# A shared expert cut at two and a half blocks of tokens, with its third block's first inner values kept on chip

## The chip, the cores and the metric

The kernel runs on one core of one Trainium2 chip. The metric is the device time of one execution in microseconds; the figure for a kernel is the median of its runs. A profile is one further execution, recorded by the hardware profiler. The core has five engines with a queue of instructions each: PE (matrix multiply; the profile shows its weight loads apart, as PEld), DVE (vector), ACT (scalar functions), POOL (GpSimd) and SP (it issues DMAs here). [...]

## The reference

Two layers, each with a residual: attention over 2 × 1024 tokens of width 256, and then a mixture of experts. The change lies in the second:

```python
def _L0_ffn_ref(hidden_states, gate_w, shared_gate_w, w13, w2, se_gate_up_w, se_down_w):
    ...
    gu = x @ se_gate_up_w.T
    I_sh = se_down_w.shape[1]
    shared = jax.nn.silu(gu[:, :I_sh]) * gu[:, I_sh:] @ se_down_w.T
    shared = shared * jax.nn.sigmoid(x @ shared_gate_w.T)
    logits = x @ gate_w.T
    probs = jax.nn.softmax(logits.astype(jnp.float32), axis=-1)
    weights, sel = jax.lax.top_k(probs, TOP_K)
    ...
    return (shared + sparse).reshape(orig_shape)
...
x = x + _L0_attn_ref(_layernorm(x, axis=-1), ...)
x = x + _L0_ffn_ref(_layernorm(x, axis=-1), ...)
```

`sparse` is the sum over 60 routed experts (inner width 176), each token going to its best 4 of them. The shared expert (inner width 704) takes every token. All of it is fp32.

## The kernel before

The 2048 tokens are 16 tiles of 128. After attention and routing, the mixture of experts runs in three stages on PE:

1. **First half of the shared expert** (the loop at L1095), for the tokens 0 to 1023, while routing of the last tiles still runs beside it.
2. **Routed experts** (L1173 to L1201): 60 experts in turn. Each reads its rows from `xg` in HBM (`rows_of`, the tile `xe`), is transposed on PE (`tpe`, copied by DVE to `xT`), multiplied (`up`, `second`), and its rows are scattered to `yt` in HBM by POOL (`send_back`, L884).
3. **The tail**, the second half of the shared expert (the loop at L1271), for the tokens 1024 to 2047. Beside it, `gather(i)` loads the four routed results of tile i (`got`, an SP DMA of 512 KB at L1263) and adds them to `acc` by four DVE instructions (L1265). Finished tiles go to the output.

The shared expert works on blocks of 512 tokens (`FB`), four in all, and `shared` takes two of them per call. For one block, `ups` makes the inner values `hs` in 6 chunks of 128 (`NC2`): two groups of matmuls per chunk (the last chunk is half as wide and needs one), 11 groups in all (L814, tile `sg`); ACT takes the silu of the first (L824), and DVE multiplies it by the second (L826). `downs` then multiplies `hs` by the second weight, for four tiles of 128 tokens (L836, tile `so`), and DVE adds each result, weighted, to `acc` (L844). Each `yield` is a step: PE has issued one group of `sg`, or one of `so`. The order for blocks a and b is ups(a), ups(b), downs(a), downs(b): 30 steps. `sg` has two PSUM buffers for each of its two halves, and `so` has two.

What else the steps carry: in the first half, the pieces of work in `later` and then `weighs` are taken up one per step for the first 22 steps, and then two per step. A piece of `later` is one scatter of a token tile's rows to `xg`: a DVE instruction makes the indices (L685), then POOL issues the indirect DMA (L690). A piece of `weighs` is four DVE instructions (L711). The last 16 scatters and 4 pieces of `weighs` fall into this loop. Expert row loads wait for all scatters. In the tail, `gather` is called in steps 4, 6, 7, 9, 10, 12, ..., two steps of every three.

The order on PE, DVE, ACT and POOL is that of the code (a manual schedule) in the first half; in the routed experts ACT, DVE and SP are manual, and in the tail PE and DVE. A manual engine takes its instructions in the order in which the Python code issues them, so that an instruction that waits holds up all behind it. What is left is put in order by a scheduler.

The pools of SBUF are two stacks, left and right, and a pool that closes gives its place to the next. In the first half `hs` has two buffers in `sw` on the left; in the tail two buffers in `sw2` on the right.

```python
        for r, _ in enumerate(shared(blocks[:half], sw, ps_sg, ps_so)):
            ...
            for _ in range(1 if r < 2 * (2 * NC2 - 1) else 2):
                if later or weighs and r >= 12:
                    (later or weighs).pop(0)()
...
        for r, _ in enumerate(shared(blocks[half:], sw, ps_sg, ps_so)):
            if r >= 4 and todo and r % 3 != 2:
                i = todo.pop(0)
                gather(i)
```

Of the kernel before, what the change touches and what calls it, by code (L numbers as in the profile page):

```python
# [1 line left out]

# [14 lines left out]
P = 128  # L17
B, T, C = 2, 1024, 256
NT = B * T // P
# [3 lines left out]
CC = C // P  # L23
# [4 lines left out]
NC2 = -(-ISH // P)  # L28
# [5 lines left out]
FB = 512  # L34
# [17 lines left out]
def attention_moe_kernel(  # L52
# [15 lines left out]
    nc = tc.nc  # L68
# [14 lines left out]
    acc = const.tile([P, NT, C], F32, name="acc")  # L83
# [35 lines left out]
    ends_of, ends_s = pool("ends", 1, "right")  # L119
# [96 lines left out]
    sg = const.tile([P, NT], F32, name="sg")  # L216
# [5 lines left out]
    start = const.tile([P, E], F32, name="start")  # L222
# [13 lines left out]
    ps_misc, ps_misc_s = pool("ps_misc", 1, space=PSUM)  # L236
# [281 lines left out]
    later = []  # L518
    exps = []
    weighs = []  # L520
# [279 lines left out]

    added = []

    def shared(blocks, sw, ps_sg, ps_so):


        def ups(n, hs):
            for m in range(NC2):
                last = m == NC2 - 1
                ps = []
                for part in range(1 if last else 2):  # L810
                    p = ps_sg.tile([P, FB], F32, tag=f"sg{part}", name=f"sg{n}_{m}_{part}")
                    c0 = (2 * m + part) * P
                    for c in range(CC):
                        nc.tensor.matmul(  # L814
                            p,
                            lhsT=ws1_sb[:, c, c0 : c0 + P],
                            rhs=x2T[:, c, n * FB : (n + 1) * FB],
                            start=c == 0,
                            stop=c == CC - 1,
                        )  # L820
                    ps.append(p)
                    if part == 0:
                        r = 64 if last else P
                        nc.scalar.activation(hs[0:r, m, :], p[0:r, :], AF.Silu)  # L824
                    if last or part == 1:
                        nc.vector.tensor_mul(  # L826
                            hs[0:r, m, :], hs[0:r, m, :], p[64:P, :] if last else p
                        )
                    yield

        def downs(n, hs):
            for t in range(FB // P):
                i = n * (FB // P) + t
                po = ps_so.tile([P, C], F32, tag="so", name=f"so{i}")
                for m in range(NC2):
                    nc.tensor.matmul(  # L836
                        po,
                        lhsT=hs[:, m, t * P : (t + 1) * P],
                        rhs=ws2_sb[:, m, :],
                        start=m == 0,  # L840
                        stop=m == NC2 - 1,
                    )
                added.append(
                    nc.vector.scalar_tensor_tensor(  # L844
                        acc[:, i, :], po, sg[:, i : i + 1], acc[:, i, :], ALU.mult, ALU.add
                    )
                )
                yield

        ahead = None  # L850
        for n in blocks:
            hs = sw.tile([P, NC2, FB], F32, tag="hs", name=f"hs{n}")
            nc.gpsimd.memset(hs[64:P, NC2 - 1, :], 0.0)
            yield from ups(n, hs)
            if ahead is not None:
                yield from downs(*ahead)
            ahead = (n, hs)
        yield from downs(*ahead)


    def up(xT, w, h, n, ps_gu, name):
# [85 lines left out]
    with tc.manual_schedule(engines={mybir.EngineType.PE}), ExitStack() as both:  # L947
# [46 lines left out]
        ahead = scores(*order[0])  # L994
        for r, (b, qb, jp, jj, s) in enumerate(order):
            if r == R // B:
# [6 lines left out]
                fc, fc_s = pool("fc", 1, "left")  # L1003
                xs = fc.tile([P, NT, XR], F32, name="xs")
                nc.gpsimd.memset(xs[:, :, C:XR], 0.0)
                x2T = fc.tile([P, CC, NT * P], F32, name="x2T")
                ws1_sb = fc.tile([P, CC, 2 * ISH], F32, name="ws1_sb")
                nc.sync.dma_start(ws1_sb, ws1.rearrange("(c p) n -> p c n", p=P))
                ws2_sb = fc.tile([P, NC2, C], F32, name="ws2_sb")
                nc.sync.dma_start(ws2_sb, ws2.rearrange("(c p) n -> p c n", p=P))  # L1010
                rw, rw_s = pool("rw", 2, "left")
# [6 lines left out]
            if r + 1 < R:  # L1018
                ahead = scores(*order[r + 1])
# [9 lines left out]
            for g in range(NKV):  # L1029
                nc.tensor.matmul(  # L1030
                    av[32 * g : 32 * g + 32, :],
                    lhsT=vaug[:, b * TPB + s, g, H * jj : H * jj + 32],
                    rhs=es[g // 2][:, g % 2, :],
                    start=s == 0,
                    stop=s == TPB - 1,
                )
            if s == TPB - 1:
                group_end(av, encT, jp, jj)
                if jp == 1 and jj == 1:
                    for t in range(0, QB // P, 2):  # L1040
                        i = (b * T + qb * QB) // P + t
# [15 lines left out]
        ps_m2, ps_m2_s = pool("ps_m2", 1, space=PSUM)  # L1057
        turns = [0]

        def bank(n, name):  # L1060
            turns[0] += 1
            of = (ps_misc, ps_m2)[turns[0] % 2]
            return of.tile([P, n], F32, tag="misc", name=name)

        sw, sw_s = pool("sw", 2, "left")
        ps_sg, ps_sg_s = pool("ps_sg", 2, space=PSUM)
        ps_so, ps_so_s = pool("ps_so", 2, space=PSUM)
# [22 lines left out]
        went = [False, False]  # L1090
        sp_s = ExitStack()
        sp_s.enter_context(tc.manual_schedule(engines={mybir.EngineType.SP}))
        blocks = range(NT * P // FB)
        half = len(blocks) // 2
        for r, _ in enumerate(shared(blocks[:half], sw, ps_sg, ps_so)):  # L1095
            if ends:
                fill(R + r)

            for k, steps in enumerate(rest):
                if r >= 3 + 3 * k and next(steps, R) == R:  # L1100
                    went[k] = True
            if all(went):
                next(ranked, None)
            for _ in range(1 if r < 2 * (2 * NC2 - 1) else 2):
                if later or weighs and r >= 12:
                    (later or weighs).pop(0)()
        assert not ends and all(went) and next(ranked, R) == R
        for piece in later + weighs:
            piece()
        sp_s.close()  # L1110
        both.close()
        rk_s.close()
        for s in (ps_so_s, ps_sg_s, ps_m2_s, ps_misc_s, sw_s, rw_s, ends_s):
            s.close()


# [56 lines left out]
        with tc.manual_schedule(  # L1173
# [12 lines left out]
            ahead = None  # L1186
            for k, r in enumerate(turn_of):
                h = hbuf[k % 3]
                up(xTs.pop(k), ws[k], h, CAPS[r], ps_gu, f"{r}")
                last = (r, ws[k], h, xes.pop(k))  # L1190
# [4 lines left out]
                ahead = last  # L1195
# [57 lines left out]


    gw, gw_s = pool("gw", 6, "right")
    sw, sw_s = pool("sw2", 2, "right")
    ps_sg, ps_sg_s = pool("ps_sg2", 2, space=PSUM)
    ps_so, ps_so_s = pool("ps_so2", 2, space=PSUM)

# [8 lines left out]

    with tc.manual_schedule(engines={mybir.EngineType.PE, mybir.EngineType.DVE}):
        todo = list(range(NT))  # L1270
        for r, _ in enumerate(shared(blocks[half:], sw, ps_sg, ps_so)):  # L1271
            if r >= 4 and todo and r % 3 != 2:
                i = todo.pop(0)
                gather(i)
                if i < TPB and i % 2:
                    nc.scalar.dma_start(ot[:, i - 1 : i + 1, :], acc[:, i - 1 : i + 1, :])
        for i in todo:
            gather(i)
    for i in range(TPB, NT):
        nc.sync.dma_start(ot[:, i, :], acc[:, i, :])  # L1280
    for s in (ps_so_s, ps_sg_s, sw_s, gw_s, fc_s):
        s.close()


# [70 lines left out]
```

## Time and profile before

| | us |
|---|---|
| median of 3 runs | 686.99 (686.0 to 687.66) |
| the profiled execution | 687.18 |
| its span | 685.1 |
| first matmul of `downs` in the first half | at 402.71 |
| first transpose of a routed expert | at 425.60 |
| first matmul of the tail | at 622.81 |
| first addition of a gathered tile (L1265) | at 631.80 |
| last DVE addition (L844) | at 681.61, takes 0.48 |

The span is what the profiler shows from the first to the last instruction; the execution's own time is 2.1 us longer. Times "at" are microseconds from the span's start. In the profile a line such as `acc<-so,sg,acc` names the tile that is written and those that are read; "x96" counts records, of which a matmul in fp32 leaves several; and what stands after `<-` behind an idle time is what ended the wait. The end of a matmul is modelled in the profile, and the profile's word for a releaser that it can't name is "remote".

### The profile page before, as it was taken

To read this page: it belongs to the slowest core of one execution; us is meant where nothing else is said; L and a number is where in the kernel's file an instruction comes from. 1 tells how busy PE (TensorE), PEld (TensorE's weight loads), DVE (VectorE), ACT (ScalarE), POOL (GpSimd) and SP (SyncE) were. 2 spreads that over 40 slices of the span, in tenths; PEclk is the share of its full clock that TensorE was granted. 3 is DMA by queue.
4 is the path that set the end of the run, shared out by engine and by line. 5 is a ranking of instruction groups with operands and counts; after the bars stand their busy time and mean duration, and the time that the engine had idled before them with its cause. 6 is when DMAs were issued, how large, how long until landed. Compare 5 with 4: busy or idle time off the path is not lost. (4 is left out here: it accounts for less than half of the span.)

```text
span 685.1 us, 12519 instructions
## 1 busy us (share of the span) xinstructions
PE 669.6 (98%) x4194; PEld 380.5 (56%) x4195; DVE 367.6 (54%) x1403; ACT 356.7 (52%) x499; POOL 190.2 (28%) x259
## 2 busy tenths in 40 slices
PE   8899999999999999999999998999999999999997
PEld 8433333332224323233225567998898889985466
DVE  4656684823035286446648764444454445443884
ACT  2567787779987687867872510333333333332110
POOL 5020100200000034433045253344544455443000
PEclk9999999999999999999999999999999999999999
DMA  8999930030000011111011076698989888933951
GB/s 283 289 284 298 333 101 1 1 132 1 1 1 1 1 42 50 66 49 59 0 58 58 16 261 229 206 290 293 311 281 295 285 287 299 293 110 105 306 178 52
DMA packets 64275, 106.33 MB, mean 155 GB/s; under 512 B 7417, under 2 KB 51209, under 8 KB 64210
## 3 DMA queue, kind: packets, MB, share of 16 engines
q1 hardware_dynamic: 55010, 86.57, 39.0%
q0 software_dynamic: 7680, 17.32, 7.4%
q10 hardware_dynamic: 1520, 1.64, 0.7%
q8 instruction: 33, 0.54, 0.3%
q14 instruction: 32, 0.26, 0.2%
HBM read 64.13 MB, written 42.45 MB: 156 GB/s over the span
## 5 line engine op out<-in xcount | busy, mean ns | idle before, releaser
L496 PE MATMUL sc<-qT,kT 32*128 32x512 f32 x1024 | 159.8, 639 | 1.9 <-DVE qT L479 0.9
L511 ACT ACTIVATE ex<-sc,rqk 128x1024 f32<-128x1024 f32 x128 | 134.4, 1111 | 37.8 <-PE sc L496 36.2
L1030 PE MATMUL av<-ex,vaug 128*32 128x512 f32 x1024 | 137.3, 604 | 2.0 <-DVE den L537 1.3
L511 ACT ACTIVATE ex<-sc 128x1024 f32<-128x1024 f32 x128 | 124.0, 1021 | 28.9 <-PE sc L496 26.0
L884 POOL DMA_INDIRECT yt<-ys,dst x96 | 93.0, 969 | 115.2 <-ACT ys L1169 75.9
L496 PEld LDWEIGHTS sc<-qT,kT 32*128 32x128 f32 x1024 | 52.4, 183 | 110.1 <-issue 68.6
L1162 PE MATMUL ye<-w,hbuf 128*128 128x256 f32 (+5 forms) x384 | 93.3, 381 | 0.0
L690 POOL DMA_INDIRECT xg<-xs,idx x64 | 63.3, 989 | 93.9 <-DVE idx L685 68.6
L814 PE MATMUL sg<-x2T,ws_sb 128*128 128x512 f32 x176 | 78.1, 596 | 1.1 <-ACTq L1240 1.1
L868 PE MATMUL gua<-xT,w 128*128 128x128 f32 (+5 forms) x480 | 73.2, 295 | 0.5 <-DVE xT L1150 0.5
L868 PEld LDWEIGHTS gua<-xT,w 128*128 128x128 f32 x480 | 70.1, 191 | 4.9 <-issue 0.6
L1169 ACT COPY ys<-ye 128x256 f32<-128x256 f32 (+5 forms) x60 | 29.9, 499 | 75.6 <-PE ye L1162 62.1
L1162 PEld LDWEIGHTS ye<-w,hbuf 128*128 128x128 f32 (+5 forms) x384 | 58.9, 164 | 14.5
L876 DVE TENSOR_TENSOR hbuf<-hbuf,gua 128x128 f32<-128x128 f32 (+5 forms) x60 | 18.9, 315 | 82.5 <-ACT hbuf L875 35.1
L1030 PEld LDWEIGHTS av<-ex,vaug 128*32 128x32 f32 x1024 | 20.4, 107 | 76.5 <-issue 66.7
L814 PEld LDWEIGHTS sg<-x2T,ws_sb 128*128 128x128 f32 x176 | 32.6, 190 | 38.9 <-issue 35.8
L875 ACT ACTIVATE hbuf<-gua 128x128 f32<-128x128 f32 (+5 forms) x60 | 18.0, 299 | 59.8 <-PE gua L868 44.6
L824 ACT ACTIVATE hs<-sg 128x512 f32<-128x512 f32 (+1 forms) x24 | 14.3, 597 | 59.2 <-PE sg L814 57.0
L424 POOL TENSOR_TENSOR t<-u,rope_sb 128x128 f32<-128x128 f32 x32 | 16.9, 558 | 99.1 <-DVE u L412 61.7
L836 PE MATMUL so<-ws_sb,hs 128*128 128x256 f32 x192 | 42.5, 381 | 1.5 <-DVE acc L844 1.5
L868 PE MATMUL gub<-xT,w 128*112 128x128 f32 (+5 forms) x240 | 41.2, 294 | 0.0
L836 PEld LDWEIGHTS so<-ws_sb,hs 128*128 128x128 f32 x192 | 36.2, 190 | 8.2 <-DVE acc L844 2.2
(182 smaller groups left out, 679.0 us busy)
## 6 DMA issues: line engine op xcount, KB each, us to landing
w<-in_wexp_dram SPq DMA_DIRECT2D x60, 624.0 KB
xg<-void SPq DMA_DIRECT2D x60, 221.0 KB
yt<-zero SPq DMA_DIRECT2D x32, 256.0 KB
got<-yt SPq DMA_DIRECT2D x16, 512.0 KB
xe<-xg SPq DMA_DIRECT2D x24, 136.0 KB
xe<-xg SPq DMA_DIRECT2D x10, 170.0 KB
yt<-ys,dst POOLq DMA_INDIRECT x96
xe<-xg SPq DMA_DIRECT2D x8, 187.0 KB
```

What stands on the lines that cost most here:

```text
L496: nc.tensor.matmul(sc[:, gg, :], lhsT=kT[b][r : r + 32, s0 : s0 + P], rhs=qT[b][r : r + 32, j, t0 : t0 + QB], start=True, stop=True,)
L511: nc.scalar.activation(ex, sc, AF.Exp, scale=rqk[:, 1, i : i + 1] if b == 0 else 1.0)
L690: s = nc.gpsimd.indirect_dma_start(out=xg[:, :], out_offset=bass.IndirectOffsetOnAxis(ap=at_, axis=0), in_=xs[:, i, :], in_offset=None, bo ...
L814: nc.tensor.matmul(p, lhsT=ws1_sb[:, c, c0 : c0 + P], rhs=x2T[:, c, n * FB : (n + 1) * FB], start=c == 0, stop=c == CC - 1,)
L836: nc.tensor.matmul(po, lhsT=hs[:, m, t * P : (t + 1) * P], rhs=ws2_sb[:, m, :], start=m == 0, stop=m == NC2 - 1,)
L868: nc.tensor.matmul(ps[part][0:m, 0:n], lhsT=w[:, c * W1C + c0 : c * W1C + c0 + m], rhs=xT[:, c, 0:n], start=c == 0, stop=c == CC - 1,)
L875: nc.scalar.activation(h[:, 0, 0:n], ps["ga"][:, 0:n], AF.Silu)
L876: nc.vector.tensor_mul(h[:, 0, 0:n], h[:, 0, 0:n], ps["ua"][:, 0:n])
L884: s = nc.gpsimd.indirect_dma_start(out=yt[:, :], out_offset=bass.IndirectOffsetOnAxis(ap=at, axis=0), in_=y, in_offset=None, bounds_check= ...
L1030: nc.tensor.matmul(av[32 * g : 32 * g + 32, :], lhsT=vaug[:, b * TPB + s, g, H * jj : H * jj + 32], rhs=es[g // 2][:, g % 2, :], start=s == 0,
L1162: nc.tensor.matmul(po[:, t, :], lhsT=h[:, k, t * rows : (t + 1) * rows], rhs=w[:, CC * W1C + k * C : CC * W1C + (k + 1) * C], start=k == 0 ...
L1169: nc.scalar.copy(ys, po)
```

## The change

`shared` is taken apart into two generators, `ups(n, chunks, ps_sg, sw)` and `downs(n, ps_so)`, which find the inner values of block n in `hs_of[n]`. The loops chain them by hand:

- First loop: ups(0), ups(1), downs(0), the first three chunks of ups(2) (six groups), downs(1): 36 steps. `later` and `weighs` are taken up one per step to the end.
- Second loop: the last three chunks of ups(2) (five groups), ups(3), downs(2), downs(3): 24 steps. `gather` is called in steps 4, 6, 7, 8, 9, 10, 12, ..., five steps of every six.

The values of block 2 lie in a pool of their own, `kept`, that stays open on the right from the first loop to the end. For it the pool `ends` stays open too, so that the pools of the routed experts start at another place. `sw2` has one buffer, for block 3. The computation, its instructions and its DMAs are the same in number and size.

```diff
+    hs_of = {}
+
+    def ups(n, chunks, ps_sg, sw):
+
+        if n not in hs_of:
+            hs = hs_of[n] = sw.tile([P, NC2, FB], F32, tag="hs", name=f"hs{n}")
+            nc.gpsimd.memset(hs[64:P, NC2 - 1, :], 0.0)
+        hs = hs_of[n]
+        for m in chunks:
...
+    def downs(n, ps_so):
+        for t in range(FB // P):
...
-        ahead = None
-        for n in blocks:
-            hs = sw.tile([P, NC2, FB], F32, tag="hs", name=f"hs{n}")
-            nc.gpsimd.memset(hs[64:P, NC2 - 1, :], 0.0)
-            yield from ups(n, hs)
-            if ahead is not None:
-                yield from downs(*ahead)
-            ahead = (n, hs)
-        yield from downs(*ahead)
...
+        kept, kept_s = pool("kept", 1, "right")
         sw, sw_s = pool("sw", 2, "left")
...
-        blocks = range(NT * P // FB)
-        half = len(blocks) // 2
-        for r, _ in enumerate(shared(blocks[:half], sw, ps_sg, ps_so)):
+
+        part = range(NC2 // 2), range(NC2 // 2, NC2)
+        steps_of = chain(
+            ups(0, range(NC2), ps_sg, sw),
+            ups(1, range(NC2), ps_sg, sw),
+            downs(0, ps_so),
+            ups(2, part[0], ps_sg, kept),
+            downs(1, ps_so),
+        )
+        for r, _ in enumerate(steps_of):
...
-            for _ in range(1 if r < 2 * (2 * NC2 - 1) else 2):
-                if later or weighs and r >= 12:
-                    (later or weighs).pop(0)()
+            if later or weighs and r >= 12:
+                (later or weighs).pop(0)()
...
-        for s in (ps_so_s, ps_sg_s, ps_m2_s, ps_misc_s, sw_s, rw_s, ends_s):
+        for s in (ps_so_s, ps_sg_s, ps_m2_s, ps_misc_s, sw_s, rw_s):
...
-    sw, sw_s = pool("sw2", 2, "right")
+    sw, sw_s = pool("sw2", 1, "right")
...
-        for r, _ in enumerate(shared(blocks[half:], sw, ps_sg, ps_so)):
-            if r >= 4 and todo and r % 3 != 2:
+        steps_of = chain(
+            ups(2, part[1], ps_sg, kept),
+            ups(3, range(NC2), ps_sg, sw),
+            downs(2, ps_so),
+            downs(3, ps_so),
+        )
+        for r, _ in enumerate(steps_of):
+            if r >= 4 and todo and r % 6 != 5:
...
```

More of the change, by code (lines that the diff above doesn't have):

```diff
@@ L1 @@
 from contextlib import ExitStack
+from itertools import chain
 import concourse.bass as bass
@@ L801, in attention_moe_kernel @@
     added = []
-    def shared(blocks, sw, ps_sg, ps_so):
-        def ups(n, hs):
-            for m in range(NC2):
[L808 to L846, printed above, removed]
-                )
-                yield
-        ahead = None
-        for n in blocks:
-            hs = sw.tile([P, NC2, FB], F32, tag="hs", name=f"hs{n}")
-            nc.gpsimd.memset(hs[64:P, NC2 - 1, :], 0.0)
-            yield from ups(n, hs)
-            if ahead is not None:
-                yield from downs(*ahead)
-            ahead = (n, hs)
-        yield from downs(*ahead)
@@ new lines, in attention_moe_kernel @@
+    hs_of = {}
[5 more added lines that the diff above has]
+        for m in chunks:
+            last = m == NC2 - 1
+            ps = []
+            for part in range(1 if last else 2):
+                p = ps_sg.tile([P, FB], F32, tag=f"sg{part}", name=f"sg{n}_{m}_{part}")
+                c0 = (2 * m + part) * P
+                for c in range(CC):
+                    nc.tensor.matmul(
+                        p,
+                        lhsT=ws1_sb[:, c, c0 : c0 + P],
+                        rhs=x2T[:, c, n * FB : (n + 1) * FB],
+                        start=c == 0,
+                        stop=c == CC - 1,
+                    )
+                ps.append(p)
+                if part == 0:
+                    r = 64 if last else P
+                    nc.scalar.activation(hs[0:r, m, :], p[0:r, :], AF.Silu)
+                if last or part == 1:
+                    nc.vector.tensor_mul(
+                        hs[0:r, m, :], hs[0:r, m, :], p[64:P, :] if last else p
+                    )
+                yield
@@ new lines, in downs @@
+    def downs(n, ps_so):
+        for t in range(FB // P):
+            i = n * (FB // P) + t
+            po = ps_so.tile([P, C], F32, tag="so", name=f"so{i}")
+            for m in range(NC2):
+                nc.tensor.matmul(
+                    po,
+                    lhsT=hs_of[n][:, m, t * P : (t + 1) * P],
+                    rhs=ws2_sb[:, m, :],
+                    start=m == 0,
+                    stop=m == NC2 - 1,
+                )
+            added.append(
+                nc.vector.scalar_tensor_tensor(
+                    acc[:, i, :], po, sg[:, i : i + 1], acc[:, i, :], ALU.mult, ALU.add
+                )
+            )
+            yield
@@ L1092, in attention_moe_kernel @@
         sp_s.enter_context(tc.manual_schedule(engines={mybir.EngineType.SP}))
-        blocks = range(NT * P // FB)
-        half = len(blocks) // 2
-        for r, _ in enumerate(shared(blocks[:half], sw, ps_sg, ps_so)):
+        part = range(NC2 // 2), range(NC2 // 2, NC2)
[5 more added lines that the diff above has]
+            downs(1, ps_so),
+        )
+        for r, _ in enumerate(steps_of):
             if ends:
@@ L1270, in attention_moe_kernel @@
         todo = list(range(NT))
-        for r, _ in enumerate(shared(blocks[half:], sw, ps_sg, ps_so)):
-            if r >= 4 and todo and r % 3 != 2:
+        steps_of = chain(
[3 more added lines that the diff above has]
+            downs(3, ps_so),
+        )
+        for r, _ in enumerate(steps_of):
+            if r >= 4 and todo and r % 6 != 5:
                 i = todo.pop(0)
@@ L1280, in attention_moe_kernel @@
         nc.sync.dma_start(ot[:, i, :], acc[:, i, :])
-    for s in (ps_so_s, ps_sg_s, sw_s, gw_s, fc_s):
+    for s in (ps_so_s, ps_sg_s, sw_s, gw_s, kept_s, ends_s, fc_s):
         s.close()
```

## The prediction

> **What bounds the kernel now.** I read the page first, then the chain of waits, then busy time by stage, then the waits and the order of time at the two places that the diff touches.
>
> ```profile
> span 685.1 us, 12519 instructions
> PE 669.6 (98%) x4194; PEld 380.5 (56%) x4195; DVE 367.6 (54%) x1403; ACT 356.7 (52%) x499; POOL 190.2 (28%) x259
> PE sg L814 6%; PE so L836 3%; DVE acc L844 0%
> ```
>
> PE, the matmul engine, is busy 98% of the span, and the chain that ends last is only the tail: L814 and L836 back to back. So the time moves in two ways alone: PE idles less somewhere, or it is made to wait somewhere new. Busy time in three stretches (the end of the shared expert's first half, the routed experts, the tail):
>
> ```profile
> core 0: us, PE busy (x) PEld busy (x) DVE busy (x) ACT busy (x) POOL busy (x), PEclk, DMA share, GB/s
> 402.70:425.80 23.10, 21.62 (x99) 18.14 (x98) 10.92 (x55) 0.59 (x1) 9.79 (x10) 1.00 0.84 302
> 425.80:621.70 195.90, 195.17 (x1296) 174.95 (x1294) 90.34 (x469) 65.07 (x179) 90.17 (x93) 1.00 0.80 259
> 622.80:681.70 58.90, 58.75 (x184) 34.88 (x184) 40.98 (x84) 7.17 (x12) 2.90 (x4) 1.00 0.56 180
> ```
>
> The routed experts leave PE 0.7 us of idle in 196: nothing to win there. The tail leaves it none, but DVE already works 41.0 of 58.9 us. The first stretch, eight `so` groups, has holes. Its waits:
>
> ```profile
> DVE acc L844 <- PE so L836: 7.9, 4, 3.7
> DVE acc L844 <- remote: 3.7, 1, 3.7
> PEld so L836 <- DVE acc L844: 2.2, 2, 1.9
> PE so L836 <- DVE acc L844: 1.5, 1, 1.5
> ```
>
> Two PSUM buffers hold `so`; a group may start when the DVE addition (L844) two groups earlier is done. The order of time shows these additions going late:
>
> ```profile
> 410.97 0.48 DVE L844 SCALAR_TENSOR_TENSOR acc<-so,sg,acc 128x256 f32<-128x256 f32 x1 [2.26 <-PE so L836]
> ...
> 415.28 0.48 DVE L844 SCALAR_TENSOR_TENSOR acc<-so,sg,acc 128x256 f32<-128x256 f32 x1 [3.68 <-remote]
> ...
> 419.62 0.48 DVE L844 SCALAR_TENSOR_TENSOR acc<-so,sg,acc 128x256 f32<-128x256 f32 x1 [3.72 <-PE so L836]
> ...
> 420.16 5.60 PE L836 MATMUL so<-ws_sb,hs 128*128 128x256 f32 x24 [1.48 <-DVE acc L844]
> ```
>
> In the tail a `so` group takes 20.73/8 = 2.59 us (in the chain of waits 96 records, eight groups, take 20.73). Counted from 402.71, group 4 ends near 413.1 and group 5 near 415.7, but their additions start at 415.28 and 419.62: they hear of them 2 to 4 us late. In just this time the DMA share is 1.0 and over (8 expert weights of 624 KB and ten scatters). The eight groups need 20.72 us and run from 402.71 to about 425.76, so 2.33 us are lost.
>
> [...] Here the last scatter ends on POOL at 418.38 and the row load that waits for it issues at 420.06: 1.7 us. [...] L826 measures 686 ns, and I use the trace's values.
>
> **The change, part by part.** Everything before 402.71 keeps its order on every engine.
>
> *Moved PE work.* Six groups of `ups(2)` leave the tail for the place between downs(0) and downs(1). A group costs 38.03/22 = 1.729 us (L814 x88, 4 records each), so 10.37 us are added in the middle and 10.37 leave the tail: PE's sum is unchanged.
>
> *The hole in the middle.* The two late signals belong to the last `so` of block 0 and the first of block 1. Between these now stand 10.37 us of matmuls that need neither buffer, so the 2.33 us go. What is late next: if silu of the first moved group also hears of it only at 419.6, its PSUM buffer comes free at about 420.2 (0.6 us of ACT), and PE wants it at 402.71 + 10.36 + 4 × 1.729 = 419.99. I take 0.3 us for this; bounds 0 and 2.3 (the same lateness landing on a buffer that is wanted at once). Downs(1) then comes after the DMA rush, with additions 2.6 us apart and at most 1.3 us of weighing (L711) between them: no wait.
>
> *Scatters.* One per step instead of two. POOL spends 0.98 us on each at a pitch of 1.28. The last index now stands on DVE behind the product of the second moved pair (PE end 420.0, product 0.7), so the last scatter issues near 421, lands near 423.3, and the row loads (`xe`) issue 3.2 us later than now. Before, they issued at 420.06 and the transposes that read them ran at 425.60, right behind the last `so`: at most 5.5 us to land. PE wants them after downs(1), near 433.9. Cost 0, hidden by 5 us. On SP the register load of the overflow count now stands ahead of these loads; its input is ready at 404.87, SP is idle until 420: 0. On POOL the three clears of `hbuf` and one of the kept `hs` (about 0.5 us each, as L853) move between scatters that wait for indices anyway: 0, at worst 2 us of those 5. The 0.50 us before the first `gua` stays, and the experts keep their order and their 8 weights already loaded: 0.
>
> *The tail.* Put T = 0 at its first matmul (622.81 before). DVE's pitches in the tail: a gather's four additions 1.957 us (eight in 646.32 to 650.23), a product 0.60, an addition of `so` 0.40:
>
> ```profile
> 646.32 4.00 DVE L1265 SCALAR_TENSOR_TENSOR acc<-got,wk,acc 128x256 f32<-128x256 f32 x8
> 650.23 0.68 DVE L826 TENSOR_TENSOR hs<-hs,sg 128x512 f32<-128x512 f32 x1
> 650.83 2.04 DVE L1265 SCALAR_TENSOR_TENSOR acc<-got,wk,acc 128x256 f32<-128x256 f32 x4
> ```
>
> The same 16 gathers must now fit a tail 10.4 us shorter, five in six steps. They can't start earlier: they wait for the routed experts' last scatter, and the first was added at 631.80, T + 8.99. Walk through it. The last kept group ends at 5 × 1.729 = 8.64, silu 0.65 and product 0.60 end at 9.97, and gather 0 runs to 11.92. The next product waits for PE until 12.17, and from there DVE does not rest: nine gathers (17.61), six products (3.60) and the first `so` addition (0.40) end at 33.78. PE has 16 × 1.729 + 2 × 2.59 = 32.84 us of work before it needs that buffer, so it waits 1.0 us. Afterwards DVE has 12 us of work in 13.6 and keeps up. PE ends at 33.84 + 6 × 2.59 = 49.4, the last addition (0.5) at 49.9. Walked in the same way, the kernel before ends at 59.2, with no wait; measured 59.28. So the tail shrinks by 9.3 to 9.4, not 10.37. Bounds of the new wait: 0.5 us if a gather takes 1.90, 1.9 if it takes 2.05 (its records without overlap). Loads don't limit: six are in flight, and at 350 GB/s (636 to 642 us) 512 KB take 1.5 us. The last output DMA is as before.
>
> *Sum.* Middle +10.37 − 2.33 + 0.3 = +8.3, tail −9.35: −1.0 us. The profiled execution took 687.18 us (2.1 around its span), which gives 686.2; it lies 0.19 above the median 686.99, so against that 686.0.
>
> **Rivals.** *DVE keeps pace:* the late signals vanish and the tail wait is nil, because gathers overlap better or the first ones start on loads that have landed sooner; −2.3: 684.7 us. For it: the walk puts only 1 us of wait, on one buffer. Against: DVE would be busy nearly all of 38 us. *The lateness moves:* what delays the signals is the DMA rush, and silu and product of the moved groups hear late too, with PSUM buffers two deep as well; middle saves nothing, tail loses 1.0: about 688.0 us, no change that can be measured. Against: these buffers are wanted 4 groups, 6.9 us, after the late moment. *DVE sets the end (slower):* the tail's gathers stand in front of products and additions in a FIFO. If gather 0 can be added later than T + 10, every further us is a us that PE waits for `so`; at T + 13.2 the wait is 4.0 us and the total 689.0 us. It decides from about T + 12.6. For it: the `hs` of block 3 and `got` now lie in memory that the experts have just used, with longer lists of waits. Against: before it was T + 8.99, with the same chain of scatters ahead.
>
> **How the numbers follow.** A measurement of this kernel tells about 0.2% (1.4 us) from no change: faster is below 685.6, slower above 688.4. My case 0.42, its own range 685.0 to 687.2 from the bounds of the two waits, of which 0.12 lies below 685.6. DVE keeps pace 0.30, lateness moves 0.13, DVE sets the end 0.15. Faster 0.42, same 0.43, slower 0.15. The range reaches from below the second case to above the third: 684.0 to 688.4.
>
> **What would show it.** Right: between the first downs and the first transpose of the experts PE has under 0.5 us of idle; the experts begin 8.0 to 8.6 us later and last as long as before; in the tail PE waits about 1 us, once, for an L849 addition at the third or fourth of the eight `so` groups, behind gathers. Wrong: PE waits on `sg` in the middle, `xe` that lands after downs(1), a first gather after T + 10, or several waits of PE on DVE in the tail.

## The result, and the profile after

| | before | after |
|---|---|---|
| median of 20 runs each, same chip, us | 686.64 (685.69 to 693.04) | 690.61 (688.87 to 696.46) |
| the profiled execution, us | 687.18 | 691.59 |
| its span, us | 685.1 | 689.7 |

The changed kernel is slower by 0.61% (ratio 1.0061, 95% interval 1.0047 to 1.0075), some 4 us. The forecast was 686.0 us, with a range from 684.0 to 688.4.

The page first: span, busy PE, and the shares of the chain that ended last, by engine and by line.

```profile
span 689.7 us, 12522 instructions
...
PE 670.7 (97%) x4194; PEld 381.9 (55%) x4195; DVE 367.6 (53%) x1403; ACT 356.2 (52%) x499; POOL 190.3 (28%) x259
...
DVE 3%; PE 3%; DMA 1%; issue 0%; ACT 0%
DVE acc L1267 2%; PE so L841 2%; DMA got<-yt 1%; PE sg L819 1%; DVE hs L831 1%; DVE acc L849 0%; ACT hs L829 0%
```

PE works 670.7 us where it worked 669.6, in a span that is 4.6 us longer: the loss is mostly waiting. And the end is no longer PE's alone. Before, the last chain was L814 and L836; now it runs through a gather's landing and its additions on DVE (L1267). (After the change L819 makes `sg`, L841 `so`, L849 adds `so`, L863 is the experts' first product, L1136 loads the rows, L1146 transposes them.)

PE in order of time, in the middle and at the start of the experts (columns: start, us busy, engine, line, operation, records, and the idle time before it):

```profile
402.41 10.52 PE L841 MATMUL so<-ws_sb,hs 128*128 128x256 f32 x48
412.77 10.46 PE L819 MATMUL sg<-x2T,ws_sb 128*128 128x512 f32 x24
423.07 10.52 PE L841 MATMUL so<-ws_sb,hs 128*128 128x256 f32 x48
433.43 0.38 PE L1146 MATMUL tpe<-ident,xe 128*128 128x128 f32 x2
436.32 0.50 PE L1146 MATMUL tpe<-ident,xe 80*128 80x80 f32 x4 [2.50 <-DMA xe<-xg]
436.65 1.64 PE L863 MATMUL gua<-xT,w 128*128 128x128 f32 x8
438.08 1.06 PE L863 MATMUL gub<-xT,w 128*112 128x128 f32 x4
```

The first three lines are what was forecast: 48, 24 and 48 records without a hole, 31.02 us in place of 22.89, +8.13. The fifth was not. The first expert's rows are there, the second expert's are not, and PE waits 2.50 us for them. The last two lines show something besides: in the kernel before, the same `gua` and `gub` take 1.13 and 0.60 us:

```profile
426.76 1.13 PE L868 MATMUL gua<-xT,w 128*128 128x128 f32 x8 [0.50 <-DVE xT L1150]
427.73 0.60 PE L868 MATMUL gub<-xT,w 128*112 128x128 f32 x4
```

Busy time in short stretches (the eighth field, behind the POOL count, is the granted clock):

```profile
core 0: us, PE busy (x) PEld busy (x) DVE busy (x) ACT busy (x) POOL busy (x), PEclk, DMA share, GB/s
...
436.00:438.00 2.00, 1.68 (x12) 1.68 (x13) 0.49 (x1) 0.00 (x0) 0.00 (x0) 0.76 0.84 214
438.00:440.00 2.00, 2.00 (x12) 2.00 (x11) 0.80 (x3) 0.55 (x2) 0.00 (x0) 0.50 0.36 100
440.00:442.00 2.00, 2.00 (x17) 2.00 (x16) 0.59 (x2) 0.46 (x2) 0.00 (x0) 0.89 0.03 8
```

The granted clock is half from 437.03 to 440.44, 3.41 us, in which PE, by that clock, does the work of 1.7 (an estimate from the length and the clock; a comparison of traces under e2_warm gives a loss of 1.6). The wait and the half clock together are 4.2 us; the 0.50 us that PE used to wait before the first `gua` no longer shows, which leaves 3.7. The whole experts' stretch, from its first transpose to the first matmul of the tail, went from 197.21 us (425.60 to 622.81) to 201.27 (433.43 to 634.70), +4.06; the rest is a wait of 0.38 us for a later expert's rows, at 546.02.

Why are the rows late? The row loads are issued by SP, in order. SP's queue waited in 400 to 440:

```profile
SPq L1136 <- PE so L841: 9.5, 1, 9.5
```

and the six loads, in order of time, spread over 12.53 us where in the kernel before they took 3.17 (first line before, second after):

```profile
420.06 3.17 SPq L1134 DMA_DIRECT2D xe<-xg  x6
423.64 12.53 SPq L1136 DMA_DIRECT2D xe<-xg  x6
```

The first load goes out at 423.64, 3.6 us later than before; the forecast had 3.2. The second waits 9.5 us, until the last `so` group is through, and leaves at 433.72, with the other four behind it. A row load has no business with `so`, except by its place in memory. The built programs give each tile's address in SBUF (bytes in a partition):

```
                   hs0              hs1              xe of 1st expert  xe of 2nd expert
before   157,536-169,824  169,824-182,112   191,968-194,144   205,024-207,200
after    157,536-169,824  169,824-182,112   163,296-165,472   176,352-178,528
```

`kept` (12,288 bytes) stays open into the tail, and so does `ends` (16,384 bytes), which was closed ahead of the experts before. Both lie on the right stack, and `ework`, the pool of `xe`, is opened above them: it has moved by their 28,672 bytes, into the place where `sw` on the left has just been. The second expert's rows now land on `hs1`, which the last `so` group reads. The third to the fifth lie on `hs1` as well. The sixth lies on `hs0`, which `downs(0)` has left at 412.93, and it still goes out last, at 435.8, in the order of SP's queue.

The tail, PE and then the first gather's additions on DVE:

```profile
634.70 27.73 PE L819 MATMUL sg<-x2T,ws_sb 128*128 128x512 f32 x64 [0.88 <-ACTq L1242]
662.27 5.34 PE L841 MATMUL so<-ws_sb,hs 128*128 128x256 f32 x24
670.10 15.81 PE L841 MATMUL so<-ws_sb,hs 128*128 128x256 f32 x72 [2.48 <-DVE acc L849]
```

```profile
646.03 2.05 DVE L1267 SCALAR_TENSOR_TENSOR acc<-got,wk,acc 128x256 f32<-128x256 f32 x4 [1.12 <-DMA got<-yt]
```

One wait, at the third `so` group, as forecast, but of 2.48 us and not 1.0. The first gather is added at T + 11.33 and not at T + 9.97, because it lands late: DVE stands idle for 1.12 us until then. Why it landed late in this execution isn't shown; in the second trace of the same kernel (e8_after_again below) DVE does not wait for it. The last addition ends at 686.43, so the tail is 51.73 us long, 7.55 shorter than before, where 9.35 was forecast. Sum: +8.13 + 4.06 − 7.55 = +4.64; the first `so` stood 0.30 us earlier in this execution, so the last addition ends 4.34 later.

### The profile page after: what moved, and what is told of

Its sections match the earlier page's. It is cut to its first block, busy times and chain, and to the rows that moved or that the text cites. A ratio compares the mean times of both kernels' runs of the same rounds, so it can differ in the third digit from the quotient of the medians.

```text
span 689.7 us, 12522 instructions
## 1 busy us (share of the span) xinstructions
PE 670.7 (97%) x4194; PEld 381.9 (55%) x4195; DVE 367.6 (53%) x1403; ACT 356.2 (52%) x499; POOL 190.3 (28%) x259
## 5 line engine op out<-in xcount | busy, mean ns | idle before, releaser
L819 PE MATMUL sg<-x2T,ws_sb 128*128 128x512 f32 x176 | 78.3, 596 | 0.9 <-ACTq L1242 0.9
L863 PE MATMUL gua<-xT,w 128*128 128x128 f32 (+5 forms) x480 | 74.1, 298 | 0.0
L863 PEld LDWEIGHTS gua<-xT,w 128*128 128x128 f32 x480 | 71.1, 193 | 4.2
L819 PEld LDWEIGHTS sg<-x2T,ws_sb 128*128 128x128 f32 x176 | 32.6, 190 | 38.2 <-issue 35.0
L841 PE MATMUL so<-ws_sb,hs 128*128 128x256 f32 x192 | 42.2, 380 | 2.5 <-DVE acc L849 2.5
L863 PE MATMUL gub<-xT,w 128*112 128x128 f32 (+5 forms) x240 | 41.7, 297 | 0.0
L841 PEld LDWEIGHTS so<-ws_sb,hs 128*128 128x128 f32 x192 | 36.4, 190 | 9.1 <-DVE acc L849 2.9
```

What stands on the lines that cost most here:

```text
L819: nc.tensor.matmul(p, lhsT=ws1_sb[:, c, c0 : c0 + P], rhs=x2T[:, c, n * FB : (n + 1) * FB], start=c == 0, stop=c == CC - 1,)
L841: nc.tensor.matmul(po, lhsT=hs_of[n][:, m, t * P : (t + 1) * P], rhs=ws2_sb[:, m, :], start=m == 0, stop=m == NC2 - 1,)
L863: nc.tensor.matmul(ps[part][0:m, 0:n], lhsT=w[:, c * W1C + c0 : c * W1C + c0 + m], rhs=xT[:, c, 0:n], start=c == 0, stop=c == CC - 1,)
```

## The experiments

Each ratio is to the kernel before on the same chip in the same session. The sessions ran on several chips, and the kernel before had different medians on them (683.77 to 686.64 us), so times of different sessions are not compared directly.

### Is it the place in memory? e1_fix and e3_before_pad

e1_fix is the change with `kept` on the left stack, in the place of `hs0`, the two `hs` of `sw` above it, and `ends` closed where it was. `ework` is then back at 191,968, and what it meets there is `hs0` (now at 182,112 to 194,400), whose last reader, `downs(0)`, is through 10.7 us before the first row load goes out. On the left stack `rw` lies under `kept`, so it stays open in place of `ends`.

```diff
-        kept, kept_s = pool("kept", 1, "right")
-        sw, sw_s = pool("sw", 2, "left")
+        kept, kept_s = pool("kept", 1, "left")
+        sw, sw_s = pool("sw", 1, "left")
+        for n in (1, 0):
+            hs_of[n] = sw.tile([P, NC2, FB], F32, name=f"hs{n}")
...
-        for s in (ps_so_s, ps_sg_s, ps_m2_s, ps_misc_s, sw_s, rw_s):
+        for s in (ps_so_s, ps_sg_s, ps_m2_s, ps_misc_s, sw_s, ends_s):
...
-    for s in (ps_so_s, ps_sg_s, sw_s, gw_s, kept_s, ends_s, fc_s):
+    for s in (ps_so_s, ps_sg_s, sw_s, gw_s, kept_s, rw_s, fc_s):
```

> The changed kernel with the same order of work, but block 2's inner values placed on the left stack, the pool ends closed as in the kernel before, and block 1's inner values placed below block 0's, so that the experts' row tiles no longer lie where block 1's inner values lay. Theory A (memory reuse): the second row load waits for the last matmul of downs(1) only because its tile lies in that memory. Then all six row loads issue within about 4 us of the last scatter (423 to 428), PE has under 0.6 us of idle before the experts, the granted clock stays at 1.000, the stretch from the first expert transpose to the first matmul of the tail falls from 201.3 to about 197.3 us, and the kernel is about 4 us shorter than the changed one: ratio to before 0.999 to 1.002. Theory B (late scatters): the loads are late because the last scatter is late; then they stay near 434, and the ratio stays at 1.006.

e3_before_pad is the reverse: the kernel before, its order untouched, with `ends` kept open and a tile of 12,288 bytes that nothing reads in place of `kept`.

```diff
+        gap, gap_s = pool("gap", 1, "right")
+        held = gap.tile([P, NC2, FB], F32, name="held")
+        nc.gpsimd.memset(held[64:P, NC2 - 1, :], 0.0)
         sw, sw_s = pool("sw", 2, "left")
...
-        for s in (ps_so_s, ps_sg_s, ps_m2_s, ps_misc_s, sw_s, rw_s, ends_s):
+        for s in (ps_so_s, ps_sg_s, ps_m2_s, ps_misc_s, sw_s, rw_s):
...
-    for s in (ps_so_s, ps_sg_s, sw_s, gw_s, fc_s):
+    for s in (ps_so_s, ps_sg_s, sw_s, gw_s, gap_s, ends_s, fc_s):
```

> The kernel before, with its own order of work, but the pool ends kept open and an unused tile of 12,288 bytes per partition held where the changed kernel keeps block 2's inner values. Theory A (memory reuse): placement alone brings the wait: the second row load issues only after the last matmul of downs(1), near 426; PE idles 2 to 3 us after the first transposes, the clock halves for 3.4 us, and the kernel becomes 3 to 4.5 us slower than before: ratio 1.004 to 1.007. Rival (the moved matmuls or the scatters' pace are to blame): no change, ratio 1.000.

Measured: e3_before_pad 688.58 us, ratio 1.0064 (1.0051 to 1.0077), 4.8 us slower than the kernel before, with no work added but one small clear. Its PE in order of time:

```profile
402.49 20.88 PE L836 MATMUL so<-ws_sb,hs 128*128 128x256 f32 x96
423.21 0.38 PE L1147 MATMUL tpe<-ident,xe 128*128 128x128 f32 x2
426.03 0.50 PE L1147 MATMUL tpe<-ident,xe 80*128 80x80 f32 x4 [2.44 <-DMA xe<-xg]
426.37 1.25 PE L868 MATMUL gua<-xT,w 128*128 128x128 f32 x8
427.41 1.06 PE L868 MATMUL gub<-xT,w 128*112 128x128 f32 x4
```

It is the same picture: first transpose, 2.44 us of waiting for the second expert's rows, and slow matmuls after it. And with the place mended in the change (e1_fix), PE in order of time:

```profile
433.66 0.66 PE L1149 MATMUL tpe<-ident,xe 128*128 128x128 f32 x6
434.82 1.13 PE L863 MATMUL gua<-xT,w 128*128 128x128 f32 x8 [0.51 <-DVE xT L1155]
...
630.25 27.73 PE L819 MATMUL sg<-x2T,ws_sb 128*128 128x512 f32 x64 [1.16 <-ACTq L1245]
657.82 5.34 PE L841 MATMUL so<-ws_sb,hs 128*128 128x256 f32 x24
664.63 15.81 PE L841 MATMUL so<-ws_sb,hs 128*128 128x256 f32 x72 [1.47 <-DVE acc L849]
```

Six transposes in one go and `gua` at 1.13 us: the wait and the half clock are gone, and the experts take 196.59 us (433.66 to 630.25). The loss in the experts is shown from both sides to be one of placement, and not of order. That e1_fix, at 686.95 us, was still 1.0058 (1.0035 to 1.008) times the kernel before refuted the expectation of 0.999 to 1.002. Something else was off, on the side of the kernel before.

### How much of it is the clock? e2_warm

The change, with 18 records of matmuls whose result nobody reads between the first and the second expert's transposes (2.17 us in its trace), so that PE stands still for 1.08 us instead of 2.50.

```diff
+            idle = ps_y.tile([P, 2, C], F32, tag="ye", name="idle")
+            for _ in range(9):
+                nc.tensor.matmul(idle[:, 0, 0:P], lhsT=ident, rhs=ident, start=True, stop=True)
             xTs[1] = turned(turn_of[1], xes[1])
```

> The changed kernel with nine dummy matmuls of 128 columns (about 2.5 us) on PE between the first and the second expert's transposes; they compute nothing that is used. Theory: the halved clock for 3.4 us after the wait comes from PE's idling and costs about 1.6 us; the dummies fill the wait, so the row load is as late as before, the clock stays at 1.000, and the kernel is 1 to 2 us shorter than the changed one: ratio to before 1.003 to 1.005. Rival: the halved clock has another cause or costs nothing: the ratio stays at 1.006 or grows.

Measured: 688.81 us, ratio 1.0070 (1.0057 to 1.0083). No half clock is left in its middle (mean clock 1.000, where the changed kernel has 0.997), and `gua` takes 1.10 us. So the half clock comes from PE standing still there: 2.50 us of it were followed by the half clock, 1.08 were not. From the start of the first `gua` to the transposes of the expert after next (72x72), e2_warm takes 3.34 us, e1_fix 3.38 and the changed kernel 5.00: the half clock costs 1.6 us in that place. By its ratio alone the run went the rival's way. The changed kernel later measured 1.0088 (1.0059 to 1.0117) on the same chip (e8_after_again below); the two intervals overlap, and in the traces the experts' stretch is only 0.70 us shorter (199.52 against 200.22), because the rows come 0.32 us later here and a later expert waits 0.32 us. That filling the wait gains 1.6 us as a whole is therefore not shown.

### The stall of the kernel before: e5_before_again, e8_after_again, e11_before_third

The forecast set 2.33 us to the change's credit for a stall between `so` groups in the trace of the kernel before. To see whether it is always there, two more traces of that kernel, and one of the changed kernel on the chip of the first.

> The kernel before, word for word, for a second trace. In the first trace TensorE stood still for 1.48 us between two so groups at 418.7 to 420.2, and the forecast takes 2.33 us back for that stretch. Theory A, the stall belongs to that one execution: here the eight so groups run through from about 402.5 to 423.3 (x96 in 20.9 us), the first tpe starts at 423.3, and the span is 682 to 683 us. Rival B, the stall belongs to the kernel before and the change removes it: again 1.3 to 2 us of idle before the last two so groups, the first tpe near 425.5, the span about 685 us.

> The changed kernel, word for word, on the chip of these experiments, for a second trace and a ratio beside the others. Theory A, the row load's wait for the last so group costs about 4 us whatever the chip and the stall of the kernel before is not there: ratio 1.007 to 1.010, again 2.4 us of idle on tpe released by DMA xe. Rival B, the ratio of 1.0061 is the same on every chip: 1.005 to 1.007.

> The kernel before, word for word, a third trace. Theory A: no stall between so groups, as in e5_before_again; first tpe 20.7 us after the first so. Rival B: the stall of the first trace comes and goes; again 1.3 us or more.

PE in order of time, e5_before_again:

```profile
402.02 20.88 PE L836 MATMUL so<-ws_sb,hs 128*128 128x256 f32 x96
422.75 0.38 PE L1144 MATMUL tpe<-ident,xe 128*128 128x128 f32 x2
```

and e11_before_third:

```profile
401.60 15.88 PE L836 MATMUL so<-ws_sb,hs 128*128 128x256 f32 x72
418.91 5.61 PE L836 MATMUL so<-ws_sb,hs 128*128 128x256 f32 x24 [1.43 <-DVE acc L844]
424.35 0.66 PE L1144 MATMUL tpe<-ident,xe 128*128 128x128 f32 x6
```

The stall comes and goes. In e5 the eight groups run through, 20.73 us, and the median of the kernel before in that session was 684.51 us (22 runs). In e11 it is there, 22.75 us from the first `so` to the first transpose, and the median of the session was 686.42 (35 runs). In the session of e1_fix it was 683.77, and e3_before_pad, which ran there, has no stall. The changed kernel doesn't follow: 690.61 us at first, and 690.47 (ratio 1.0088, 1.0059 to 1.0117) in the session of e5, where its trace has the wait for the second expert's rows again, 2.77 us. That fits a kernel before that loses 2 us on some chips and not on others, and a changed kernel that has no such loss in either session. What decides about the stall isn't shown, and one trace for each session is little.

With e5 as its partner, e1_fix falls into place. Middle 31.02 against 20.73 us, +10.29; experts 196.59 against 196.56; tail 50.70 against 59.27, −8.57. That is +1.7 us, and e1_fix's first `so` came 0.62 later: 2.4 of the 2.7 us between the spans. Moving six groups from one stretch that PE fills to another brings nothing where there is no stall to fill; here it costs 1.7 us.

### The scatters alone: e6_scatter_one

```diff
-            for _ in range(1 if r < 2 * (2 * NC2 - 1) else 2):
-                if later or weighs and r >= 12:
-                    (later or weighs).pop(0)()
+            if later or weighs and r >= 12:
+                (later or weighs).pop(0)()
```

> Before, with one scatter per step in place of two in the so groups; some six scatters are then recorded after the last so group. It is the scatter part of the change alone. Theory A, this part costs nothing, because POOL works through its scatters at 1.3 us each whatever their place in the program: ratio 0.998 to 1.001. Rival B, the last scatters now stand behind all of the so additions on DVE, the xg rows and the first row loads come about 3 us later, and TensorE waits for xe: ratio 1.003 to 1.006 and an idle on tpe released by DMA xe.

Measured: 693.56 us, ratio 1.013 (1.0089 to 1.0171), more than either theory gave. PE and POOL in order of time:

```profile
401.77 20.88 PE L836 MATMUL so<-ws_sb,hs 128*128 128x256 f32 x96
428.31 0.69 PE L1143 MATMUL tpe<-ident,xe 128*128 128x128 f32 x2 [5.66 <-DMA xe<-xg]
```

```profile
418.33 0.98 POOL L690 DMA_INDIRECT xg<-xs,idx  x1 [1.61 <-DVE idx L685]
420.93 0.98 POOL L690 DMA_INDIRECT xg<-xs,idx  x1 [1.61 <-DVE idx L685]
423.51 0.98 POOL L690 DMA_INDIRECT xg<-xs,idx  x1 [1.61 <-DVE hit L711]
```

With one scatter per step the scatters come every 2.59 us, the time of a `so` group, and not every 1.28: each one's index is made on DVE behind that step's `so` addition. The last issues at 423.51 (in e5 at 416.13), the row loads follow at 426.20, and PE waits 5.66 us at once, 7.2 in all over the experts. The clock falls to half at 425.68, still within this wait, and stays there for 10.24 us. In the change this part is free only because ten microseconds of other PE work now stand ahead of the experts: in e1_fix the last scatter issues at 421.17 and the rows are there at 433.66.

### The tail: e7_fix_less, e9_fix_tail

Is it DVE as a whole that is too slow for the shorter tail, or only what stands ahead of the first `so` additions? e7_fix_less is e1_fix without the gathers of the last two tiles.

```diff
-        todo = list(range(NT))
+        todo = list(range(NT - 2))
```

> The change with block 1's and block 0's hs put where the row loads do not wait (as in e1_fix), and with the gathers of the last two of the 16 token tiles left out, 4.1 us of DVE work. Theory A, in the changed tail DVE sets the end by a little: e1_fix had its first gather at T+10.1 and needed 40.6 us from there, against 49.0 us of TensorE work from T. Without two gathers the wait of the so group goes, and the tail comes down from 50.7 to 49.2 to 49.5 us: e7_fix_less is 1.2 to 1.5 us faster than e1_fix, which makes a ratio of 1.001 to 1.004 to the kernel before. Rival B, DVE sets the whole of the tail: 4 us faster than e1_fix, ratio 0.998 to 1.000. Rival C, the tail is TensorE's alone: no gain, ratio 1.005 to 1.007.

e9_fix_tail is e1_fix with all 16, but with nine gathers ahead of the first `so` addition in place of ten:

```diff
-            if r >= 4 and todo and r % 6 != 5:
+            if r >= 4 and todo and r not in (5, 11, 15):
```

> e1_fix with one gather fewer ahead of the so groups of the tail: the steps without a gather are 5, 11 and 15 in place of 5, 11 and 17. All 16 gathers are there. Theory A: the 1.47 us in which TensorE waits for the so addition are DVE's backlog of gathers at that point alone, so the wait goes, the tail from its first matmul to the last so addition comes down from 50.2 to 48.8 us, and the ratio to the kernel before is 0.999 to 1.003. Rival B: the gather that is moved behind makes the later so additions late by as much, the wait comes back there, and the tail stays at 50.2 us, ratio 1.002 to 1.006. Nothing under 0.998 is expected of either: the moved sg groups cost the middle 10.3 us and relieve the tail of 10.3 us.

Measured: e7_fix_less 686.39 us, ratio 1.0023 (1.0008 to 1.0038), as the expected theory had it; but its trace shows the rival C in the tail. The wait is still 1.47 us, and the tail 50.70 us long, exactly that of e1_fix. The ratio fell into the expected range by luck: e1_fix's own median of six contains two runs at a mean clock of 0.992, and its other four (685.39 to 687.49 us) lie around the median of e7_fix_less. Work left out behind the wait does nothing for it. e9_fix_tail, PE in order of time:

```profile
631.18 27.73 PE L819 MATMUL sg<-x2T,ws_sb 128*128 128x512 f32 x64 [1.16 <-ACTq L1245]
658.76 20.88 PE L841 MATMUL so<-ws_sb,hs 128*128 128x256 f32 x96
```

96 records without a wait: one gather fewer ahead, 2.0 us of DVE, is enough. Of the 1.47 us only 0.54 is gained (tail 50.16 us), because now DVE is last: PE ends at 679.6, and the last `so` addition, behind the last gather, starts at 680.86 (49.68 us after the tail's first matmul, where theory A had 48.8). So the wait was of one place, and behind it DVE has little in hand too. e9_fix_tail took 685.12 us, ratio 0.9989 (0.9974 to 1.0004), in the session in which the kernel before stalls (e11); it was not run on the chip of e1_fix. It and e10_fix_tail_two below are the only forms of the change that came out level with the kernel before.

### One chunk, two chunks, and the spread of e1_fix: e4_fix_one, e12_two_chunks, e10_fix_tail_two

e4_fix_one is e1_fix with one chunk moved (two `sg` groups), two scatters per step from step 28, and the tail's old density of gathers. e12_two_chunks moves two chunks (four groups), with one scatter per step.

```diff
-        part = range(NC2 // 2), range(NC2 // 2, NC2)
+        part = range(1), range(1, NC2)
...
-            if later or weighs and r >= 12:
-                (later or weighs).pop(0)()
+            for _ in range(1 if r < 28 else 2):
+                if later or weighs and r >= 12:
+                    (later or weighs).pop(0)()
...
-            if r >= 4 and todo and r % 6 != 5:
+            if r >= 4 and todo and r % 3 != 2:
```

> The placement of the first kernel of this call, but one chunk (two groups) of block 2 moved instead of three, scatters two per step from step 28, and gathers in two steps of three as in the kernel before. Theory C (the tail is bounded by DVE): the hole of 2.3 us in the middle is covered by 3.5 us of moved matmuls, and the tail, 3.5 us shorter instead of 10.4, leaves DVE enough room, so PE waits for no addition: about 2 us shorter than before, ratio 0.996 to 0.998. Rival: the hole was the profiler's, or one chunk does not cover it: ratio 0.999 to 1.001.

```diff
-        part = range(NC2 // 2), range(NC2 // 2, NC2)
+        part = range(2), range(2, NC2)
...
-            if r >= 4 and todo and r % 6 != 5:
+            if r >= 4 and todo and r not in (5, 11, 17, 20):
```

> e9_fix_tail with two chunks of block 2 moved (four sg groups, 6.9 us of TensorE work) in place of three, and no gather in steps 5, 11, 17 and 20 of the 26 in the tail. In e9_fix_tail the last so group ended at 679.6 but the last so addition, behind the last gather, at 681.3: about 1.1 us in which DVE set the end. Theory A: with 3.5 us more of TensorE work in the tail DVE keeps pace to the end, so e12 is 0.5 to 1.1 us faster than e9_fix_tail against the kernel before, on a chip where the kernel before has its stall of 1.4 us between the so groups: ratio 0.996 to 0.9985 there; where the kernel before has no stall (as in e5_before_again) 0.999 to 1.002. Rival B: with four sg groups between them the first and second so groups still fall into the DMA rush, the stall of the kernel before comes back in the middle, ratio 1.000 to 1.003 on either chip.

Both missed. e4_fix_one: 686.38 us, ratio 1.0037 (1.0025 to 1.005). Its PE has no wait in the tail. But with gathers in two steps of three the sixteenth falls to the very last step, behind the last `so` addition on DVE, and runs from 679.16 to 681.2 when PE has been done since 678.6. e12_two_chunks: 687.0 us, ratio 1.0035 (1.0022 to 1.0047), in a session in which the kernel before took 684.58. PE waits twice. In the tail it is 1.26 us, since the new list puts eleven gathers ahead of the first `so` addition. In the middle it is 1.68 us, before the first `gua`, and DVE shows why:

```profile
431.97 0.28 DVE L712 SCALAR_TENSOR_TENSOR hit<-slot,at,cw 128x60 f32<-128x60 f32 x1
432.17 0.08 DVE L712 DVE_READ_ACCUMULATOR hit<-slot,at,cw 128x1 f32 x1
432.17 0.82 DVE L1155 COPY xT<-tpe 128x256 f32<-128x256 f32 x2
```

The pieces of `weighs` (L712), taken up one per step over 34 steps in place of 36, run on into the experts, and the copies that the first expert needs stand behind them.

e10_fix_tail_two asks what made two of the six runs of e1_fix take 690 us at a mean clock of 0.992, against 685.4 to 687.5 for the others. It is e9_fix_tail with two scatters per step from step 28, which brings the row loads forward.

> e9_fix_tail with two scatters per step from step 28 on, so that the last scatter and the first row loads are recorded earlier again. Theory A: the slower runs of e1_fix and e7_fix_less (688 to 690 us at a granted clock of 0.992 to 0.995) come from row loads that are late now and then; with the loads earlier they are gone, as in e4_fix_one whose five runs lay within 1.3 us, and the ratio is 0.999 to 1.001. Rival B: the row loads have time enough in e1_fix (they are issued 9.8 us before TensorE wants them), the slower runs have another cause and stay: same median as e9_fix_tail within 0.5 us.

Measured: 685.56 us, ratio 0.9991 (0.9979 to 1.0003), the same as e9_fix_tail, and runs with a mean clock of 0.992 to 0.995 are still among its 22. The profile fell on one of them, span 688.4, and shows where the clock goes; it is far from the change (columns as above):

```profile
25.00:28.00 3.00, 2.12 (x12) 1.02 (x12) 2.65 (x9) 1.11 (x4) 0.00 (x0) 0.54 0.91 284
28.00:31.00 3.00, 3.00 (x12) 0.76 (x6) 0.20 (x2) 2.84 (x3) 0.00 (x0) 0.50 0.92 284
31.00:34.00 3.00, 3.00 (x14) 2.67 (x13) 0.00 (x0) 1.40 (x2) 0.00 (x0) 0.50 0.91 284
```

It is at half from 25.26 to 35.50, after short waits of PE at the start of the attention (0.56, 0.65 and 0.95 us, and a fourth of 0.88 that lies across the drop). That part is the same in both kernels, and e9_fix_tail (mean clock 0.999) has the same waits without a drop; the last section comes back to this. Some runs of the kernel before have a mean clock of 0.994 or 0.995. Rival B held.

## Where the prediction was right and where it failed

*The failed step* is "*Scatters.* … Cost 0, hidden by 5 us", with its "the experts keep their order and their 8 weights already loaded: 0". It timed when the scatters land and when PE wants the rows, and took for granted that six loads leave one after the other, as in the kernel before. They don't: the second load waits 9.5 us for the last `so` group, since its destination has moved onto `hs1`. The stretch cost +4.06 us where 0 stood; 2.5 us is the wait, 1.7 the half clock behind it, 0.4 a later expert's wait, less 0.5 that went. In the second pair of traces (e8_after_again against e5) it is 200.22 against 196.56 us, +3.66. That place in memory makes this loss, and alone makes it, is shown by e3_before_pad (+4.8 us without any reordering) and e1_fix (197 us again). The diff had it in sight: `ends_s` leaves the list of pools that close ahead of the experts. And the forecast named the right kind of trouble at the wrong place: its fourth case spoke of longer lists of waits for `hs` of block 3 and `got`, not for `xe`, the first tile that is loaded into the moved pool. Whether `kept` or `ends` alone would do it wasn't tried; by their sizes each would push the bottom of `ework` below the end of `hs1` (to 179,680 or 175,584 against 182,112).

*Scatters themselves:* right, and nearer to the edge than it read. They are hidden; but e6_scatter_one shows that their price without the moved groups is about 9 us, and that it comes from DVE's order (a scatter every 2.59 us, behind DVE's index), not from POOL's rate (0.98 us each).

*Moved PE work and the hole:* right for the execution that it was read from, +8.13 against +8.3, and no wait on `sg`: the 0.3 us set aside for one were not needed, and the hole was 2.16 us (22.89 against the 20.73 of e5), not 2.33, because the forecast set the groups' modelled end against a length counted from start to start. But this hole is a credit that not every session gives. Where the kernel before runs through (e5) the middle costs +10.29. The one trace that was read could not tell this.

*The tail:* the mechanism was right (one wait, third `so` group, DVE behind its gathers), and the term was mis-sized: −7.55 where −9.35 stood. The wait was 2.48 us for 1.0, since the first gather landed at T + 11.33. With the first gather at T + 10.1 (e1_fix, e8_after_again) the wait is 1.47, and the tail 50.70 us against the 49.9 forecast: 0.47 for the wait, and some 0.3 because a stop costs more than the idle time before it: broken in two, the records of the eight `so` groups take 5.34 + 15.81 = 21.15 us, in one piece 20.88. The sentence "Afterwards DVE has 12 us of work in 13.6 and keeps up" was too easy: e9_fix_tail shows DVE last by a microsecond as soon as PE doesn't wait.

*The rivals:* "DVE sets the end" came true in part and late (T + 11.33 where it was to decide from T + 12.6); it explains 1.8 of the 5.6 us between the forecast's −1.0 and the measured +4.6 of the sum. "The lateness moves" was refuted: DVE's additions in the middle start at 2.6 us intervals. The list of what would show it wrong had the right entry, "`xe` that lands after downs(1)"; no price had been put on it.

With the experts' wait taken out and the tail's mended too, what is measured is near the forecast's −1.0. e9_fix_tail, on a chip with the stall, is 0.75 us faster than the kernel before by its ratio, an interval that holds zero.

## What to carry to other kernels

When a pool stays open longer, list what is allocated above it afterwards, and for each tile that is filled by an early DMA ask who read that memory last: here one load that waited 9.5 us for the last reader held the four behind it on SP. Moving six groups between two stretches that PE fills brought only the idle time that they covered (+8.13 us in the middle where there was a stall, +10.29 where there was none), so look at more than one trace before counting a stall as a gain. And on DVE, in program order, it was the work ahead of the critical addition that had to become less: one gather fewer ahead of it (2.0 us) took away the wait of 1.47 us in e9_fix_tail, and two gathers left out behind it changed nothing in e7_fix_less.

## What was not expected of the hardware

An idle of 2.4 to 2.8 us ahead of the second expert's transposes was followed by the half clock in the changed kernel (2.50), in e8_after_again (2.77) and in e3_before_pad (2.44); the 2.48 us in the changed kernel's tail (667.62 to 670.10) were not. The half clock lasts 3.41 us in the changed kernel (437.03 to 440.44) and 3.4 in e3_before_pad (from 427.2), and 10.24 us, three times that, in e6_scatter_one (from 425.68) and in e10_fix_tail_two (25.26 to 35.50).

PE did not stand still for all of the time ahead of a drop: in the changed kernel the 3.41 us from 433.61 to 437.02 held 0.91 us of its work. The idle time of PE in the 3.41 us ahead of the drop was 2.50 us there, 2.28 in e3_before_pad and 3.03 in e6_scatter_one (estimates from the times of the waits and of the drops in these traces). In e10_fix_tail_two it was 1.7, made up of several short waits at the start of the attention; in e9_fix_tail the same waits left the clock full. Single waits of 1.48 us (the stall in the first trace of the kernel before, mean clock 1.000), of 1.47 (the tail of e1_fix, 0.999) and of 1.08 (e2_warm, 1.000) were followed by no half clock.

So in these traces the length of a wait doesn't decide alone: of two waits of 2.5 us in one execution, one was followed by the half clock and the other was not. What decides isn't shown. The one at the start of the experts cost 1.6 us more than its length. This is read from traces that were there; no run varied the length or the place of a wait on purpose to find out.
